# A graph-attention layer on one core: a table with its axes exchanged, set-up work in another order, and the last passes written out as a list

## The chip, the core and the metric

The kernel runs on one core of one Trainium2 chip. The engines of the core work side by side, each through its own queue in order: TensorE (PE; its weight loads are listed apart as PEld), VectorE (DVE), ScalarE (ACT), GpSimd (POOL) and SyncE (SP), which here only issues DMAs. The metric is the device time of one execution in microseconds (us), as the median of several runs.

## What is computed

The reference normalizes each of the 12,500 rows of x (128 numbers), lets each node look at its incoming edges (200,000 in all, sorted by target), keeps the 16 best-scored edges of a node, takes a softmax over them, and adds up the sources' rows with these weights:

```python
h = relu(layernorm(x))
Qv, Ku = h @ W_Q.T, h @ W_K.T
score = einsum('md,md->m', Qv[dst], Ku[src]) / sqrt(d) * exp(-edge_weight)
keep  = rank of the edge among those of its node < 16
w     = where(keep, exp(score - seg_max[dst]), 0)
alpha = w / segment_sum(w, dst)[dst]
agg   = segment_sum(alpha * (h[src] @ W_msg.T), dst)
out   = x + relu(h @ W_self.T + agg)
```

## The kernel before

**Groups.** The edges are cut into 112 groups (`G`) of 14 chunks of 128 edges (`GC` = 14; a 15th chunk is shared with the next group, `NJ` = 15). The last group, number 111, has 9 chunks. A group belongs to a window of at most 128 nodes. For each chunk POOL gathers 128 source rows with one indirect DMA into the tile `hs` (L176).

**Set-up (L278 to L421).** x is loaded in six pieces; DVE takes each row's statistics (`row_stats`, L194), ACT scales and clips each row block (`normed`, L215, the instructions of L220), and SP writes the piece to the table `h_tab` in DRAM (`finish`, L342). Only a complete `h_tab` can be gathered from. So that POOL need not wait for it, the first four groups (`RAW` = 4, "raw groups") are gathered from x itself (L339), and are normalized later in SBUF, inside the main loop (`raw_stats`, `raw_normed`). Before that the source indices must be turned from rows to columns: a copy (L335), PE transposes (L272), a cast into `idx_all` (L338). The groups from 4 on are gathered from `h_tab`; DVE copies two indices at a time (`let_go`, L183, the copy of L191) and POOL issues the two gathers.

**The places' table.** `pd` (L155) holds for each edge two numbers of 16 per group, the edge's place among its node's edges and its node's distance; its axes are (128 edges, group, 2, 16). DVE fills one half (L397), ACT the other (L400, L401). In each pass of the loop PE loads one group's 32 numbers as weights (L547, `edges_turned`); the copy `pdT` on ACT (L550) follows, and the matmuls into the same PSUM bank `a` (L534) wait for that copy.

**The loop (L712).** One pass `i` works on several groups at different stages, written out by hand: the scores of group `i` (PE `q_to_edges` L574, then DVE `scores` L583, `scores_in_slots` L591), the matrices for group `i+1` (`far_of`, `away`), the best 16 of group `i-2` (`slots_by_node` L599, `best`, `kept_to_edges` L642, `on_edges`), the weights and weighted sums of group `i-3` (`weights` L664, `sums` L674), the output of groups `i-4` and `i-5`. The calls `more(k)` between the stages are the `let_go` of later groups. The loop runs from -3 to `G + 5`; a stage whose group does not exist is left out. So the last seven passes (111 to 117) work the pipeline empty, in the same order as any other pass. An engine executes its instructions in the order in which the stages are written.

**Buffers that matter here.** `hs` has 8 buffers, `q` 3, the PSUM tiles `a`, `e`, `x` and `so` one each. `raw_stats` uses one set of small tiles for all raw groups.

Of the kernel before, what the change touches and what calls it, by code (L numbers as in the profile page):

```python
# [10 lines left out]
F32 = mybir.dt.float32  # L11
BF16 = mybir.dt.bfloat16
# [8 lines left out]
P = 128  # L21
# [35 lines left out]
def lead(j):  # L57
    return STEP * j - PRE
# [18 lines left out]
def gnn_layer(  # L77
# [35 lines left out]
    assert G > TAIL  # L113
# [41 lines left out]
    pd = const.tile([P, G, 2, 16], BF16, name="pd")  # L155
    dlw = pd[:, :, 1, 0:NJ]
# [58 lines left out]
    def normed(rows, n, rs, sm):  # L215

        nc.vector.reciprocal(rs, rs)
        nc.vector.scalar_tensor_tensor(sm, sm, -0.5, rs, op0=OP.mult, op1=OP.mult)
        for t in range(n):
            nc.scalar.activation(rows[:, t, :], rows[:, t, :], AF.Relu, bias=sm[:, t:t + 1],  # L220
                                 scale=rs[:, t:t + 1])

# [17 lines left out]
    with tc.tile_pool(name="edges", bufs=1) as ep, ExitStack() as stage:  # L240
# [48 lines left out]
        make_identity(nc, ident)  # L289
        nc.gpsimd.iota(dst_r, pattern=[[1, RL + P]], base=1 << 21, channel_multiplier=0)  # L290
# [3 lines left out]
        for p0, p1 in sixteens(1, k):  # L294
# [4 lines left out]
        nc.gpsimd.iota(slots, pattern=[[1, KM]], base=0, channel_multiplier=0,  # L299
                       allow_small_or_imprecise_dtypes=True)  # L300
        nc.gpsimd.iota(nvec, pattern=[[0, 1]], base=0, channel_multiplier=1,
                       allow_small_or_imprecise_dtypes=True)

        jj, eq = (alz[0][0:32, NJ * KM * k:NJ * KM * (k + 1)].rearrange("p (j k) -> p j k", k=KM) for k in range(2))
        nc.gpsimd.iota(jj, pattern=[[1, NJ], [0, KM]], base=0, channel_multiplier=0,
                       allow_small_or_imprecise_dtypes=True)
# [9 lines left out]
        nc.vector.memset(pd, 1.0)  # L316
        nc.vector.memset(dec_all[:, RR * CPR:CW], 0.0)
        nc.vector.tensor_scalar(minus, nvec, -1.0, None, op0=OP.mult)
        for j in range(NJ):
            nc.vector.memset(w0[:, j:j + 1], float(lead(j)))  # L320
# [8 lines left out]
        nc.vector.memset(alz[0], 0.0)  # L329
        for k in range(2):  # L330
            nc.vector.memset(sl1[k][:, :, KM:], 1.0)


        src_f = src_r.bitcast(F32)[:, 0:RW]
        nc.vector.tensor_copy(src_f, src_r[:, 0:RW])  # L335
        stat = {0: row_stats(prep, xs[0][2], sizes[0], "x0")}
        by_chunk = lambda t: t[:, 0:RR * CPR].rearrange("e (p j) -> e j p", j=CPR)
        to_columns(src_f, 0, lambda at, p: nc.vector.tensor_copy(at(by_chunk(idx_all)), p))  # L338
        for g in range(min(RAW, G)):  # L339
            gather_at_once(g, x)  # L340

        def finish(i):  # L342
            t0, n, xg = xs[i]
            normed(xg, n, *stat[i])
            for a, b in cuts:
                nc.sync.dma_start(by_part(h_tab)[a:b, t0:t0 + n, :], xg[a:b])

        for i in range(len(xs)):
            if i + 1 < len(xs):
                stat[i + 1] = row_stats(prep, xs[i + 1][2], sizes[i + 1], f"x{i + 1}", lambda: finish(i))  # L350
            else:
                finish(i)

# [28 lines left out]
        let_go(RAW, 2)  # L382
        nc.vector.memset(h0[:, 0:1], 0.0)
# [3 lines left out]
        let_go(RAW, 4)  # L387
        bb = rows_pool.tile([P, 2, G], F32, name="bb")
        nc.vector.tensor_copy(bb, pb[:, 0:2 * G].rearrange("p (a g) -> p a g", a=2))

        for j0 in range(0, NJ, 4):
            j1 = min(j0 + 4, NJ)
            pt = bank("q", 3)
            for j in range(j0, j1):
                nc.tensor.matmul(pt[:, (j - j0) * RR:(j - j0 + 1) * RR], lhsT=rel[:, j * P:(j + 1) * P],
                                 rhs=upper(ident[0:RR, 0:RR]), start=True, stop=True)
            nc.vector.tensor_tensor(dlw.rearrange("e g j -> e j g")[:, j0:j1, :],  # L397
                                    pt[:, 0:(j1 - j0) * RR].rearrange("e (j g) -> e j g", g=RR),
                                    bc(w0[:, j0:j1], RR), op=OP.subtract)
        to_columns(h1, HALO, lambda at, p: nc.scalar.copy(at(pd[:, :, 0, :].rearrange("e g j -> e j g")), p))  # L400
        nc.scalar.copy(pd[:, 0:G - 1, 0, GC:NJ], pd[:, 1:G, 0, 0:1])  # L401
# [30 lines left out]
    def all_checked():  # L432
# [15 lines left out]
        lambda: nc.vector.tensor_reduce(badc[:, 0:1], pd[:, :, 0, 0:NJ], axis=AX.XY, op=OP.max),  # L448
# [32 lines left out]
    with tc.tile_pool(name="win", bufs=2) as win:  # L481
# [23 lines left out]
        def raw_stats(g):  # L505
            T[g]["raw"] = row_stats(rows_pool, T[g]["hs"], own[g], "r")

        def raw_normed(g):
            normed(T[g]["hs"], own[g], *T[g]["raw"])


# [10 lines left out]
        def q_out(g):  # L522
            T[g]["q"] = win.tile([P, D], F32, name="q", bufs=3)
            nc.scalar.copy(T[g]["q"], so[:, P:2 * P])
# [20 lines left out]
        def edges_turned(g):  # L545
            pr = bank("a", 1)
            nc.tensor.matmul(pr[0:32, 0:P], lhsT=pd[:, g, :, :].rearrange("e w j -> e (w j)"), rhs=upper(ident),  # L547
                             start=True, stop=True)
            T[g]["pdT"] = win.tile([32, P], BF16, name="pdT")
            nc.scalar.copy(T[g]["pdT"], pr[0:32, 0:P])  # L550
# [161 lines left out]
        for i in range(-3, G + 6):  # L712
# [5 lines left out]
            if i + 1 < RAW:  # L718
                at(i + 1, raw_stats)

# [29 lines left out]
            if i + 1 < RAW:  # L750
                at(i + 1, raw_normed)
# [28 lines left out]
            at(i, scores_in_slots)  # L780
            more(6)
            at(i - 1, node_by_slots)
            at(i + 2, q_made)
            if i > 0 and later:
                later.pop(0)()
    assert not later
# [182 lines left out]
```

## Time and profile before

| | us |
|---|---|
| median of 10 runs | 2869.69 (2864.47 to 2878.52) |
| the profiled execution's own time | 2862.99 |
| its span, first to last instruction | 2861.2 |

| engine | busy us | share of the span | instructions |
|---|---|---|---|
| PE | 1946.3 | 68% | 13800 |
| PEld | 1546.9 | 54% | 13801 |
| DVE | 1278.9 | 45% | 6998 |
| ACT | 1053.4 | 37% | 2198 |
| POOL | 1498.6 | 52% | 1580 |

No engine is busy throughout. The rows with "idle before" tell what an engine waited for: the name after the arrow is the instruction whose signal came last, "remote" is a signal for which the profile shows no sender at that moment, and "issue" means that no wait is shown. A timeline row holds start, duration, engine, source line, operation and tiles, and behind it in brackets the idle time before. A row of windows holds a stretch of time and each engine's busy time in it, with the number of instructions, the granted PE clock as a share of the full one, the DMA engines' busy share and the rate in GB/s. The granted clock is 0.764 over the whole execution.

### The profile page before, as it was taken

To read this page: it belongs to the slowest core of one execution; us is meant where nothing else is said; L and a number is where in the kernel's file an instruction comes from. 1 tells how busy PE (TensorE), PEld (TensorE's weight loads), DVE (VectorE), ACT (ScalarE), POOL (GpSimd) and SP (SyncE) were. 2 spreads that over 40 slices of the span, in tenths; PEclk is the share of its full clock that TensorE was granted. 3 is DMA by queue.
4 is the path that set the end of the run, shared out by engine and by line. 5 is a ranking of instruction groups with operands and counts; after the bars stand their busy time and mean duration, and the time that the engine had idled before them with its cause. 6 is when DMAs were issued, how large, how long until landed. Compare 5 with 4: busy or idle time off the path is not lost. (4 is left out here: it accounts for less than half of the span.)

```text
span 2861.2 us, 42100 instructions
## 1 busy us (share of the span) xinstructions
PE 1946.3 (68%) x13800; PEld 1546.9 (54%) x13801; DVE 1278.9 (45%) x6998; ACT 1053.4 (37%) x2198; POOL 1498.6 (52%) x1580
## 2 busy tenths in 40 slices
PE   0257776776777767777776776776777777777676
PEld 0135555555555555555555555555555555555565
DVE  5436544444444444444444444444444444444445
ACT  5444333333333333333333333333333333333342
POOL 6634555555555555555555555555555555555520
PEclk9998777777777777777777777777777777777788
DMA  8211211111111111111111111111111111111110
GB/s 220 87 29 32 59 45 47 47 47 47 46 48 47 48 48 47 46 46 46 46 46 47 47 46 46 48 48 48 48 46 47 47 48 47 44 47 46 48 29 7
DMA packets 101472, 143.46 MB, mean 50 GB/s; under 512 B 31063, under 2 KB 74327, under 8 KB 100480
## 3 DMA queue, kind: packets, MB, share of 16 engines
q0 software_dynamic: 50144, 102.74, 12.6%
q1 hardware_dynamic: 51102, 37.99, 4.8%
q8 instruction: 108, 1.77, 0.3%
q14 instruction: 118, 0.97, 0.1%
HBM read 126.79 MB, written 14.40 MB: 49 GB/s over the span
## 5 line engine op out<-in xcount | busy, mean ns | idle before, releaser
L176 POOL DMA_INDIRECT hs<-h_tab,ix x1507 | 1433.1, 951 | 1234.2 <-DVE prod L583 579.0
L674 PE MATMUL a<-hs,alz 128*128 128x128 f32 x3348 | 594.3, 344 | 46.6 <-issue 43.8
L574 PEld LDWEIGHTS q<-q,to_e 128*128 128x128 f32 x3348 | 543.4, 242 | 133.1 <-issue 123.0
L534 PE MATMUL a<-rel,ident 112*128 112x512 bf16 (+1 forms) x447 | 181.4, 406 | 634.0 <-ACT far L536 580.2
L574 PE MATMUL q<-q,to_e 128*128 128x128 f32 x3348 | 591.2, 331 | 0.0
L536 ACT ACTIVATE far<-a,minus 128x512 bf16<-128x512 f32 (+1 forms) x447 | 295.2, 660 | 794.7 <-remote 590.1
L583 DVE SCALAR_TENSOR_TENSOR prod<-hs,dec_all,q 128x128 f32<-128x128 f32 x1674 | 483.2, 344 | 224.2 <-PE a L674 174.4
L674 PEld LDWEIGHTS a<-hs,alz 128*128 128x128 f32 x3348 | 547.3, 254 | 30.2 <-issue 21.6
L599 PEld LDWEIGHTS e<-opo,sl 128*41 128x41 f32 x3348 | 188.3, 140 | 679.5 <-issue 670.7
L613 DVE TENSOR_SCALAR ell<-slots,e 128x40 f32<-128x40 f32 x112 | 28.1, 251 | 1061.3 <-PE e L599 993.0
L559 ACT ACTIVATE aw<-a 128x400 bf16<-128x400 f32 x336 | 169.3, 504 | 231.1 <-PE a L557 213.7
L599 PE MATMUL e<-opo,sl 128*41 128x40 f32 x3348 | 230.2, 230 | 0.0
L557 PE MATMUL a<-minus_at,pdT 32*128 32x400 bf16 x336 | 164.8, 491 | 89.4 <-ACT aw L559 45.4
L679 ACT ACTIVATE agn<-a,rden 128x128 f32<-128x128 f32 x112 | 41.2, 368 | 443.4 <-PE a L674 438.6
L541 ACT ACTIVATE to_e<-far 128x1920 f32<-128x1920 bf16 x112 | 200.4, 1789 | 0.0
L583 DVE DVE_READ_ACCUMULATOR prod<-hs,dec_all,q 128x1 f32 x1674 | 137.9, 82 | 0.0
L563 ACT ACTIVATE opo<-aw 128x1200 f32<-128x1200 bf16 x112 | 136.0, 1215 | 0.0
L191 DVE COPY ix<-idx_all 128x2 int32<-128x2 int32 x754 | 135.1, 193 | 0.0
L642 PEld LDWEIGHTS <-to_e 128*128 128x128 bf16 x1674 | 66.9, 114 | 85.8 <-DVE prod L583 64.1
L550 ACT CAST pdT<-a 32x128 bf16<-32x128 f32 x112 | 28.5, 255 | 176.3 <-PE a L547 157.7
L591 DVE TENSOR_TENSOR sl<-opo,s 128x600 f32<-128x600 f32 x112 | 87.7, 783 | 3.8
L664 DVE TENSOR_TENSOR alz<-opo,kept 128x600 f32<-128x600 f32 x112 | 87.7, 783 | 3.9
(172 smaller groups left out, 1654.5 us busy)
## 6 DMA issues: line engine op xcount, KB each, us to landing
hs<-h_tab,ix POOLq DMA_INDIRECT x1507
h_r<-h_tab SPq DMA_DIRECT2D x112, 64.0 KB
x_t<-in_x_dram SPq DMA_DIRECT2D x108, 64.0 KB
out_dram<-o SPq DMA_DIRECT2D x108, 64.0 KB
xg<-in_x_dram SPq DMA_DIRECT2D x2, 1400.0 KB
h_tab<-xg SPq DMA_DIRECT2D x2, 1400.0 KB
xg<-in_x_dram SPq DMA_DIRECT2D x1, 1120.0 KB
h_tab<-xg SPq DMA_DIRECT2D x1, 1120.0 KB
```

The source lines that it names most:

```text
L176: nc.gpsimd.indirect_dma_start(out=T[g]["hs"][:, j, :], out_offset=None, in_=table[0:N, :], in_offset=bass.IndirectOffsetOnAxis(ap=index(j ...
L191: nc.vector.tensor_copy(ix[:, j0:j1], idx_all[:, GC * g + j0:GC * g + j1])
L534: nc.tensor.matmul(pr[:, 0:n1 - n0], lhsT=upper(ident[0:RR, g:g + 1]).to_broadcast([RR, P]), rhs=rel[:, n0:n1], start=True, stop=True)
L536: nc.scalar.activation(T[g]["far"][:, n0:n1], pr[:, 0:n1 - n0], AF.Square, bias=minus)
L541: nc.scalar.activation(T[g]["to_e"][:, 0:n], T[g]["far"][:, 0:n], AF.Relu, bias=1.0, scale=-1.0)
L557: nc.tensor.matmul(pr[:, 0:400], lhsT=T[g]["pdT"], rhs=minus_at.rearrange("k w j s -> k (w j s)")[:, n0:n1], start=True, stop=True)
L559: nc.scalar.activation(T[g]["aw"][:, n0:n1], pr[:, 0:400], AF.Square)
L563: nc.scalar.activation(T[g]["opo"].rearrange("e w j s -> e (w j s)"), T[g]["aw"], AF.Relu, bias=1.0, scale=-1.0)
L574: nc.tensor.matmul(pq[:, (j - j0) * P:(j - j0 + 1) * P], lhsT=T[g]["to_e"][:, j * P:(j + 1) * P], rhs=T[g]["q"], start=True, stop=True)
L583: nc.vector.scalar_tensor_tensor(prod, rows_of(g, j), dec_all[:, c:c + 1], T[g]["pq", b][:, (j % 4) * P:(j % 4 + 1) * P], op0=OP.mult, op1 ...
L599: nc.tensor.matmul(et[0:KM + 1, STEP * j:STEP * j + WN], lhsT=sl1[g % 2][:, j, :], rhs=T[g]["ow"][:, j, :], start=False, stop=(j == n - 1))
L674: nc.tensor.matmul(T[g]["pa"][:, 0:P], lhsT=alz[g % 2][:, WW * j + PRE:WW * j + PRE + P], rhs=rows_of(g, j), start=(j == 0), stop=(j == n ...
```

## The change

1. `pd` becomes (128 edges, 32, group): one number of all groups lies side by side, and one group's 32 numbers lie 224 bytes apart. Only the two columns that need a value beforehand are set to one, and the last group's missing places to zero.
2. In the set-up the `iota` instructions for `slots`, `nvec` and `jj` come before that of `dst_r`; the copy of the source indices is split in two; the statistics of x's first piece come after the casts to `idx_all` and the raw gathers; the fills of `w0`, `alz[0]` and `sl1` come after the last piece of x.
3. The statistics of raw groups 0 and 1 are taken right after the last piece of x, and their norming on ACT goes behind two later `let_go`. The statistics of raw groups 2 and 3 move to the end of pass 0, with the norming of the first chunk of each; the other 13 chunks are normed at the end of passes 1 and 2.
4. `q` has 2 buffers.
5. The loop ends after pass 110. Passes 111 to 117 are one list of stages (`L` = 111) in a new order.

```diff
-    pd = const.tile([P, G, 2, 16], BF16, name="pd")
-    dlw = pd[:, :, 1, 0:NJ]
+    pd = const.tile([P, 32, G], BF16, name="pd")
+    dlw = pd[:, 16:16 + NJ, :].rearrange("e j g -> e g j")
...
-    def normed(rows, n, rs, sm):
+    def normed(rows, n0, n1, rs, sm):
-        nc.vector.reciprocal(rs, rs)
-        nc.vector.scalar_tensor_tensor(sm, sm, -0.5, rs, op0=OP.mult, op1=OP.mult)
-        for t in range(n):
+        if n0 == 0:
+            nc.vector.reciprocal(rs, rs)
+            nc.vector.scalar_tensor_tensor(sm, sm, -0.5, rs, op0=OP.mult, op1=OP.mult)
+        for t in range(n0, n1):
...
+    def raw_stats(g):
+        T[g]["raw"] = row_stats(rows_pool, T[g]["hs"], own[g], f"r{g % 2}")
+    def raw_normed(g):
+        normed(T[g]["hs"], 0, own[g], *T[g]["raw"])
+    def raw_begun(g):
+        normed(T[g]["hs"], 0, 1, *T[g]["raw"])
+    def raw_finished(g):
+        normed(T[g]["hs"], 1, own[g], *T[g]["raw"])
...
-        nc.vector.memset(pd, 1.0)
+        for k in (15, 31):
+            nc.vector.memset(pd[:, k, :], 1.0)
+        nc.vector.memset(pd[:, GC:NJ, G - 1:G], 0.0)
...
-        nc.vector.tensor_copy(src_f, src_r[:, 0:RW])
-        stat = {0: row_stats(prep, xs[0][2], sizes[0], "x0")}
+        nc.vector.tensor_copy(src_f[:, 0:4 * P], src_r[:, 0:4 * P])
+        nc.vector.tensor_copy(src_f[:, 4 * P:], src_r[:, 4 * P:RW])
         to_columns(src_f, 0, lambda at, p: nc.vector.tensor_copy(at(by_chunk(idx_all)), p))
-        for g in range(min(RAW, G)):
+        for g in range(RAW):
             gather_at_once(g, x)
+        stat = {0: row_stats(prep, xs[0][2], sizes[0], "x0")}
...
+        for j in range(NJ):
+            nc.vector.memset(w0[:, j:j + 1], float(lead(j)))
+        nc.vector.memset(alz[0], 0.0)
+        for k in range(2):
+            nc.vector.memset(sl1[k][:, :, KM:], 1.0)
+        for g in range(2):
+            raw_stats(g)
...
         let_go(RAW, 2)
+        raw_normed(0)
...
         let_go(RAW, 4)
+        raw_normed(1)
...
-            nc.tensor.matmul(pr[0:32, 0:P], lhsT=pd[:, g, :, :].rearrange("e w j -> e (w j)"), rhs=upper(ident),
+            nc.tensor.matmul(pr[0:32, 0:P], lhsT=pd[:, :, g], rhs=upper(ident),
...
-        for i in range(-3, G + 6):
+        for i in range(-3, G - 1):
...
-            if i + 1 < RAW:
-                at(i + 1, raw_stats)
...
-            if i + 1 < RAW:
-                at(i + 1, raw_normed)
...
             at(i, scores_in_slots)
+            if i == 0:
+                raw_stats(2)
+                raw_stats(3)
+                raw_begun(2)
+                raw_begun(3)
+            if i in (1, 2):
+                raw_finished(i + 1)
...
+        q_to_edges(L, 0)
+        output(L - 5)
+        store(L - 5)
+        weights(L - 3)
+        turned(L - 4)
+        all_slots(L - 1)
+        slots_out(L - 1)
+        best(L - 2)
+        sum_of_exps(L - 2)
+        q_to_edges(L, 1)
+        node_by_slots(L - 1)
+        to_rows(L - 4)
+        all_sums(L - 3)
+        kept_to_edges(L - 2)
+        best(L - 1)
+        sum_of_exps(L - 1)
+        scores(L, 0)
+        kept_on_edges(L - 2)
+        turned(L - 3)
+        kept_to_edges(L - 1)
+        scores(L, 1)
+        weights(L - 2)
+        all_sums(L - 2)
+        to_rows(L - 3)
+        for b in range(2, blocks):
+            q_to_edges(L, b)
+            scores(L, b)
+        scores_in_slots(L)
+        to_nodes(L)
+        kept_on_edges(L - 1)
+        turned(L - 2)
+        best(L)
+        sum_of_exps(L)
+        weights(L - 1)
+        kept_to_edges(L)
+        all_sums(L - 1)
+        to_rows(L - 2)
+        kept_on_edges(L)
+        turned(L - 1)
+        weights(L)
+        all_sums(L)
+        to_rows(L - 1)
+        turned(L)
+        to_rows(L)
```

The new helpers put old stages together: `turned` is `sums_turned` and `sums_turned_out`; `all_slots` the three parts of `slots_by_node`; `to_nodes` is `all_slots`, `slots_out` and `node_by_slots`; `kept_on_edges` is `one_over_sum`, `on_edges` and `exps`; `all_sums` both parts of `sums` and `sums_out`; `to_rows` is `products`, `output` and `store`.

## The prediction

> **What bounds the kernel now.** I read the stretches of the span first, then the costliest groups, then the waits, then the timeline of the first 235 us and of the last 40. The stretches, with the busy time of PE, PEld, DVE, ACT and POOL in each:
>
> ```profile
> 12.00:100.00 88.00, 7.16 (x37) 5.54 (x37) 44.15 (x173) 43.17 (x109) 55.73 (x56) 1.00 0.69 192
> 100.00:147.00 47.00, 15.07 (x51) 8.73 (x52) 17.59 (x74) 26.04 (x40) 34.11 (x34) 1.00 0.22 62
> 221.00:235.00 14.00, 12.36 (x118) 9.94 (x118) 11.54 (x55) 8.44 (x17) 0.02 (x1) 1.00 0.04 11
> 235.00:2741.00 2506.00, 1785.42 (x12662) 1421.22 (x12661) 1106.20 (x6183) 895.89 (x1852) 1368.27 (x1442) 0.74 0.16 47
> 2811.00:2849.00 38.00, 26.14 (x243) 23.89 (x242) 19.34 (x90) 4.61 (x20) 4.22 (x4) 0.91 0.03 10
> ```
>
> 2506 of 2861 us are 103 ordinary passes (4 to 106) of 24.3 us. Their code is untouched but for the weights load of the places' table. One pass without gathers (221 to 235) took 14.0. The difference is seen in the groups:
>
> ```profile
> L176 POOL DMA_INDIRECT hs<-h_tab,ix x1507 | 1433.1, 951 | 1234.2 <-DVE prod L583 579.0
> L536 ACT ACTIVATE far<-a,minus 128x512 bf16<-128x512 f32 (+1 forms) x447 | 295.2, 660 | 794.7 <-remote 590.1
> ```
>
> ACT loses 590 us at L536, 105 times some 5.6 us: PE's matmuls for it are done by 1507, but the signal comes at 1512.3, 1.1 us after POOL's eighth gather in a row ended (1511.2). The same shows at 146.56 below, 1.7 us after a row of gathers that ended at 144.9. So I read a pass as POOL's: 14 gathers at 1.25 us spacing are 17.5 us, the rest are POOL's pauses. The change touches neither, so its worth lies before 235 us and after 2811. The rows there:
>
> ```profile
> 2.71 3.04 DVE L316 MEMSET pd<- 128x3584 bf16 x1 [0.69 <-issue]
> 9.69 2.06 DVE L329 MEMSET alz<- 128x2400 f32 x1 [0.57 <-DMA xg<-in_x_dram]
> 14.55 2.82 DVE L338 CAST idx_all<-q 128x448 int32<-128x448 f32 x4
> 15.75 1.12 POOL L176 DMA_INDIRECT hs<-in_x_dram,idx_all  x1 [9.57 <-DVE idx_all L338]
> 81.75 0.25 DVE L217 RECIPROCAL rsx<-rsx 125x15 f32<-125x15 f32 x1 [12.29 <-remote]
> 88.33 2.46 POOL L176 DMA_INDIRECT hs<-in_x_dram,idx_all  x1 [0.30 <-issue]
> 97.25 7.46 DVE L397 TENSOR_TENSOR pd<-q,w 128x448 bf16<-128x448 f32 x4
> 100.73 0.95 POOL L176 DMA_INDIRECT hs<-h_tab,ix  x1 [9.94 <-issue]
> 102.39 7.06 ACT L400 CAST pd<-q 128x448 bf16<-128x448 f32 x4 [7.09 <-issue]
> 108.92 1.01 ACT L401 COPY pd<-pd 128x111 bf16<-128x111 bf16 x1
> 122.06 5.48 ACT L220 ACTIVATE hs<-hs,smr,rsr 128x128 f32<-128x128 f32 x14
> 146.56 0.35 DVE L583 SCALAR_TENSOR_TENSOR prod<-hs,dec_all,q 128x128 f32<-128x128 f32 x1 [10.41 <-remote]
> ```
>
> And one row of the waits between 100 and 235 us (total, times, longest), with three of the last passes:
>
> ```profile
> PE a L557 <- ACT aw L559: 20.8, 6, 5.4
> ...
> 2817.11 3.59 PE L674 MATMUL a<-hs,alz 128*128 128x128 f32 x30
> 2826.17 4.80 PE L674 MATMUL a<-hs,alz 128*128 128x128 f32 x30
> 2834.90 5.22 PE L674 MATMUL a<-hs,alz 128*128 128x128 f32 x30
> ```
>
> The reader is to see: raw gathers start at 15.75 and end at 90.8; the first gather from `h_tab` waits until 100.73 for the table; group 0's scores wait until 146.56; and the norming of a raw group (5.48) sits between two ACT copies for which PE waits.
>
> **Indices first.** SP's queue, which reuses the semaphores of the four source loads, goes on at 6.8 to 8.7, so the indices are there by 8.7; DVE copies them at 11.71, behind the zeroing of L329. Without it (2.06) and without L316 (3.04), and with 512 of 1792 columns copied first (1.07 x 512/1792 = 0.31), the casts start at about 9.9 instead of 14.55 and the gathers at 11.1: 4.6 earlier, ending near 86. That is no gain by itself: what follows is the table. It is complete when ACT has normed x's six pieces and SP's last write has landed. ACT works at 1.4 us spacing from 51 to 92, while POOL gathers without pause, instead of the 0.39 of L220's 5.48 for 14. If POOL ends 4.6 earlier, ACT's last five rows run fast; but POOL also starts earlier to slow it. I take -3 for the first gather from `h_tab`, bounds -5 (all of it follows) and +4 (the slowing also moves forward). On POOL the three small `iota` (0.98 together) now hold up that of `dst_r`; SP loads over it only at 34.3, so nothing waits.
>
> **DVE and ACT before the loop.** DVE gets, behind x's last reciprocal, two sets of statistics (each 14 x 0.2 = 2.8 and six small ones, 108.06 to 111.77 = 3.7), the zeroing of 2.06 and 17 small fills of some 0.06: 10.5 more. It loses most of L397: 448 numbers side by side cost about 0.6, nearest row the 512 of L536 at 0.69, so 2.4 for four against 7.46: -5. ACT gets two normings, 11.0 more, filling an idle stretch of 7.1 before L400, and loses 7.06 - 2.5 at L400 and 0.8 at L401. By this the last of these tables (`dec_all`, 114.1 before) is done at about 117: +3 (0 to +5). Pass -1 then lacks its norming (-5.5), so group 0's scores could start earlier than before by 2.5; but they start when POOL pauses, 34 gathers after the first from `h_tab` (100.73 + 44 = 144.9). So only the -3 above counts here; the rest has that wait as cover, some 10 us. SP's queue keeps its order, but its writes of `h_tab` and loads of nodes follow the same table.
>
> **Passes 0 to 3.** The wait row of 100 to 235 us gives PE 20.8 us behind L559, the norming in the way: 5.2 of it in pass -1, under the cover just named, 15.6 in passes 0 to 2. PE waits for ACT's `pdT`, which stood behind the statistics' square root, 21.2 us in the same window, of which one wait of 14.4 is the late signal: 6.8 more. Removed: 22.4. Added: behind pass 0 the DVE work of two groups (7.4) stands before two square roots and two rows on ACT, and `pdT` of the next pass behind these, with about 2 us of PE work ahead of the wait: 7. DVE's `let_go` for the next pass are queued behind it, so POOL pauses too. Behind passes 1 and 2, 13 rows of 0.39 each = 5.1, of which 1.5 is ACT's usual idle time before `pdT`: 3.5 each. Added: 14. Sum -8.5, bounds -16 (the late signals hide what is added) and 0 (what was removed was hidden, what is added is not).
>
> **The turned table in the passes.** L547 loads 32 numbers in 92 ns; now each is 224 bytes from the next. The trace shows no such load. Below: nothing, it can't fall. Above: L401 reads and writes with wide steps, 9.1 ns a number, L400 writes so, 3.9; the difference of 5.2 x 32 = 0.17 us, 112 times 19 us. I take 0: the load comes before the late signal of its pass, which POOL ends, so a small delay has 5 us of cover. L430 and L444 read the table once each with the same steps, at most 1680 x 5.2 ns = 8.7 us on DVE, which waits 10.4 in each pass for L599. Two `q` buffers cost nothing: PE reads a `q` a pass before ACT overwrites it.
>
> The Trainium skill speaks against this edit (SBUF — State Buffer, section on the DMA port swizzle): it has 16-byte lines and says that each access that crosses to a new line pays. No row here shows that for weights; it gives no price, and if it meant the 0.17 above the sum would be 19 higher.
>
> **The last passes.** From the start of pass 111 (2810.9) to the end of the last store (2848.9) are 38.0. I put both orders together from rows at PE's quick speed: `sums` 3.6 (2.2 for group 111), `best` 2.0, `on_edges` with its reciprocal 2.5 (2.0), `weights` 1.0 (0.7), four scores 1.15. Old order: `sums`(109) ends at 19.5, `best`(111) at 23.5, `sums`(110) at 27.6 with `on_edges`(111) under it, `sums`(111) at 31.5, store at 34.9. New order: `best`(110) and `sums`(108) earlier (7.4, 8.6), `weights`(109) 13.7, `sums`(109) 17.3; but DVE's output of 108 stands before the last scores of 111, so these end at 18.7, `on_edges`(110) at 21.8, `best`(111) 23.8, `weights`(110) 24.8, `sums`(110) 28.5, output of 109 at 29.4, and only then `on_edges`(111) 31.4, `weights` 32.1, `sums` 34.3, store 37.7. That is 2.8 later; what both lack to 38.0 is slow PE after idle time (4.80 and 5.22 for 3.59) and the POOL queue. I take +3, bounds -1 (the new order keeps PE quick) and +6 (three slow sums).
>
> **Sum.** -3 - 8.5 + 0 + 3 = -8.5 against the profiled execution's 2863.0 = 2854.5. That execution lay 6.7 under the median of the runs shown, so for a median I say 2861.
>
> **Rivals.**
> 1. The weights load becomes dear (other side). Place L547, price up to +19, 2880; it decides from 0.13 us a pass, where 2861 + 14.4 passes 2875.4. For: ACT's and DVE's wide steps cost two to three times (L397, L401). Against: 5 us of cover in each pass. 0.12.
> 2. The set-up's gain is hidden: the table's completion and POOL's 56 gathers to group 7 set the time until pass 3. Then 0 and the list's +3: 2873. For: 146.56 follows POOL. Against: the 15.6 us lie after that point. 0.24.
> 3. The list is better than I worked out, because PE stays quick and DVE overtakes: PE's 26.1 busy us and 4 for the last output would make 30 instead of 38, so 2861 - 3 - 8 = 2850. For: idle PE in a third of the stretch. Against: the chain above. 0.14.
> 4. The passes' phase against the late signals shifts, as 22.6 to 26.5 us long passes show: 0.1 us in 103 passes is +-10, 2851 or 2871. 0.08.
>
> The forecast (2853 to 2869) has 0.42. 0.2% is about what a measurement of this kernel can tell from no change: 2864.0 to 2875.4 is the same. Faster: 0.34 of the forecast, 0.14 of rivals 3 and half of 4 = 0.52. Same: 0.08 of it and 0.18 of rival 2 = 0.26. Slower: rival 1, 0.06 of rival 2, half of 4 = 0.22. The range 2845 to 2879 leaves the dearest loads and the best list out.
>
> **What would show it.** First raw gather near 11; first from `h_tab` at 96 to 99; L397's four in 2.5 us; passes 4 to 106 at 24.3; L547's load at 0.09 to 0.12; group 3's scores done near 223.5 instead of 235; the last store 41 us after the start of group 111's first matmul. It would be wrong if passes 4 to 106 differ by 0.1 us, or if group 0's scores start later than 147.

## The result, and the profile after

The changed kernel takes 2880.46 us (median of 18 runs, 2873.06 to 2894.7) where the kernel before took 2869.36 beside it (61 runs): a ratio of 1.0043, 95% interval 1.0032 to 1.0054. It is slower by 11.1 us; the forecast was faster by 8.5 and the range ended at 2879. The profiled execution has a span of 2876.3 us where that of before had 2861.2.

The stretches of the span (start:end, length, then busy time and instructions of PE, PEld, DVE, ACT and POOL, the PE clock, the DMA share, GB/s), the first two at the same times as before, the others cut at the same places of the work:

```profile
12.00:100.00 88.00, 2.36 (x8) 1.74 (x8) 40.04 (x218) 43.16 (x111) 53.05 (x56) 1.00 0.69 191
100.00:147.00 47.00, 16.78 (x70) 11.18 (x71) 15.57 (x49) 24.69 (x52) 37.02 (x33) 1.00 0.21 59
236.00:2749.00 2513.00, 1800.51 (x12670) 1435.26 (x12668) 1107.53 (x6188) 895.89 (x1854) 1368.64 (x1442) 0.73 0.16 47
2818.00:2864.00 46.00, 32.61 (x248) 29.61 (x247) 19.31 (x91) 5.19 (x22) 3.96 (x4) 0.74 0.03 8
```

The reader is to see that no stretch became shorter: the end of pass 3 moved from 235 to 236, the passes' stretch grew from 2507 (235 to 2742) to 2513, and the last passes, 38.0 from group 111's first matmul to the last store before, now need 45.4 (2818.65 to 2864.02), with more PE busy time (32.6 for 26.1) at a lower clock (0.74 for 0.91). The two groups shown of before changed little, so a pass is built as it was:

```profile
L176 POOL DMA_INDIRECT hs<-h_tab,ix x1507 | 1439.8, 955 | 1241.0 <-DVE prod L598 593.3
L551 ACT ACTIVATE far<-a,minus 128x512 bf16<-128x512 f32 (+1 forms) x447 | 295.1, 660 | 808.6 <-remote 617.6
```

Rows of the timeline (start, duration, engine, line, operation, tiles, idle time before) that answer to those of before:

```profile
10.41 1.12 POOL L176 DMA_INDIRECT hs<-in_x_dram,idx_all  x1 [4.05 <-DVE idx_all L349]
...
98.40 0.15 DVE L191 COPY ix<-idx_all 128x2 int32<-128x2 int32 x1
98.53 1.19 DVE L399 CAST dst_r<-dst_r 112x1984 f32<-112x1984 int32 x1
98.82 2.29 POOL L176 DMA_INDIRECT hs<-h_tab,ix  x1 [14.28 <-DVE ix L191]
99.76 1.22 DVE L401 TENSOR_SCALAR rel<-dst_r 112x1920 bf16<-112x1920 f32 x1
101.33 2.09 DVE L405 TENSOR_TENSOR src_r<-dst_r 112x1855 f32<-112x1855 f32 x1
101.42 2.82 POOL L176 DMA_INDIRECT hs<-h_tab,ix  x1 [0.30 <-issue]
103.46 4.02 DVE L407 TENSOR_TENSOR_SCAN h<-src_r 112x1856 f32<-112x1856 f32 x1
104.55 3.69 POOL L176 DMA_INDIRECT hs<-h_tab,ix  x1 [0.31 <-issue]
108.11 2.09 DVE L419 TENSOR_TENSOR pd<-q,w 128x448 bf16<-128x448 f32 x4
108.54 0.95 POOL L176 DMA_INDIRECT hs<-h_tab,ix  x1 [0.30 <-issue]
...
155.70 0.69 ACT L551 ACTIVATE far<-a,minus 128x512 bf16<-128x512 f32 x1 [6.91 <-remote]
157.23 0.94 POOL L176 DMA_INDIRECT hs<-h_tab,ix  x1 [6.70 <-DVE ix L191]
```

The raw gathers start 5.3 us earlier (15.75 before) and the table's DVE writes take 2.09 instead of 7.46 (forecast 2.5). But the first gather from `h_tab` is only 1.9 earlier, it now waits for DVE's copy at 98.40, and the first three gathers take 2.29, 2.82 and 3.69 where others take 0.95, each beside a long DVE instruction. The fourth starts at 108.54 where before it started at 104.48. POOL then gathers to 150.5 without a pause, and at 155.70 ACT goes on after 6.9 us of idle time that ended with a signal of no shown sender. Such waits, "remote" in the rows, are called late signals here as in the prediction.

The weights load of the table, before (L547) and turned (L562; ns: min/median/max), and the last passes' `sums`:

```profile
L547 PEld LDWEIGHTS <-pd x112: 92/92/102, 115.0 to 2796.9; 128*32 128x32 bf16 x112
L547 PE MATMUL a<-ident,pd x112: 230/230/290, 115.0 to 2796.9; 128*32 128x128 bf16 x112
L562 PEld LDWEIGHTS <-pd x112: 134/135/138, 120.2 to 2804.5; 128*32 128x32 bf16 x112
L562 PE MATMUL a<-ident,pd x112: 217/273/324, 120.2 to 2804.5; 128*32 128x128 bf16 x112
```

```profile
2823.14 3.51 PE L689 MATMUL a<-hs,alz 128*128 128x128 f32 x30
2831.53 6.06 PE L689 MATMUL a<-hs,alz 128*128 128x128 f32 x30 [2.24 <-DVE alz L679]
2844.45 6.41 PE L689 MATMUL a<-hs,alz 128*128 128x128 f32 x30 [0.39 <-DVE alz L679]
```

The load takes 135 ns where it took 92 before, its matmul 273 where it took 230. Two of the long `sums` take 6.1 and 6.4 us instead of 3.5.

### The profile page after: what moved, and what is told of

It is laid out like the page before. It is cut to its first block, busy times and chain, and to the rows that moved or that the text cites. A ratio compares the mean times of both kernels' runs of the same rounds, so it can differ in the third digit from the quotient of the medians.

```text
span 2876.3 us, 42113 instructions
## 1 busy us (share of the span) xinstructions
PE 1968.1 (68%) x13800; PEld 1567.8 (55%) x13801; DVE 1274.4 (44%) x7001; ACT 1048.0 (36%) x2198; POOL 1502.6 (52%) x1580
## 5 line engine op out<-in xcount | busy, mean ns | idle before, releaser
L549 PE MATMUL a<-rel,ident 112*128 112x512 bf16 (+1 forms) x447 | 182.0, 407 | 661.2 <-ACT far L551 605.8
L589 PEld LDWEIGHTS q<-q,to_e 128*128 128x128 f32 x3348 | 549.7, 244 | 119.7 <-issue 104.8
L589 PE MATMUL q<-q,to_e 128*128 128x128 f32 x3348 | 598.3, 334 | 0.0
L551 ACT ACTIVATE far<-a,minus 128x512 bf16<-128x512 f32 (+1 forms) x447 | 295.1, 660 | 808.6 <-remote 617.6
L689 PEld LDWEIGHTS a<-hs,alz 128*128 128x128 f32 x3348 | 554.8, 257 | 31.2 <-issue 19.0
L572 PE MATMUL a<-minus_at,pdT 32*128 32x400 bf16 x336 | 165.2, 492 | 57.0 <-ACT aw L574 30.1
```

What stands on the lines that cost most here:

```text
L549: nc.tensor.matmul(pr[:, 0:n1 - n0], lhsT=upper(ident[0:RR, g:g + 1]).to_broadcast([RR, P]), rhs=rel[:, n0:n1], start=True, stop=True)
L551: nc.scalar.activation(T[g]["far"][:, n0:n1], pr[:, 0:n1 - n0], AF.Square, bias=minus)
L572: nc.tensor.matmul(pr[:, 0:400], lhsT=T[g]["pdT"], rhs=minus_at.rearrange("k w j s -> k (w j s)")[:, n0:n1], start=True, stop=True)
L589: nc.tensor.matmul(pq[:, (j - j0) * P:(j - j0 + 1) * P], lhsT=T[g]["to_e"][:, j * P:(j + 1) * P], rhs=T[g]["q"], start=True, stop=True)
L689: nc.tensor.matmul(T[g]["pa"][:, 0:P], lhsT=alz[g % 2][:, WW * j + PRE:WW * j + PRE + P], rhs=rows_of(g, j), start=(j == 0), stop=(j == n ...
```

## The experiments

The first eight runs, e17 and the comparison above fell on chips where the kernel before takes 2863 to 2870. The others fell on three chips where it takes 2059 to 2061; what those show is told last, since a pass takes 17 us there instead of 24.3. Three places are read from each profile: when the scores of a group are multiplied into slots ("group 0's scores", "group 4's"), the length from group 4's to group 106's ("passes 4 to 106"), and from group 110's to the end of the span ("the end"). Figures in brackets behind a ratio are its 95% interval.

**Parts of the change taken back or made alone.** e1 takes back part 5, the list:

```diff
-        for i in range(-3, G - 1):
+        for i in range(-3, G + 6):
...
-        q_to_edges(L, 0)
...
-        to_rows(L)
```

> The changed kernel with the old last passes in place of the list. Theory A (the list itself costs about 7 us: from the scores of group 110 to the end the changed kernel took 58.9 us where the kernel before took 51.5, with two sums of 6.1 and 6.4 us): about 2873, 1.0015 times before, and 51 to 52 us from group 110's scores to the end. Rival (the list is no worse; its end fell on a bad stretch of TensorE's clock that any order would meet): 2880, 1.004, and 57 us or more.

Measured: 1.0028 [1.0012, 1.0044], 4 us less than the changed kernel in ratio; the end takes 54.7 us, with two `sums` at 6.3 and 6.2. Between the two forecasts: the list costs about 4 by this run, and slow `sums` at the end also meet the old order.

e2 takes back part 1, the table's layout, but keeps its smaller fill:

```diff
-    pd = const.tile([P, 32, G], BF16, name="pd")
+    pd = const.tile([P, G, 2, 16], BF16, name="pd")
...
+        nc.vector.memset(pd[:, :, :, 15:16], 1.0)
...
-            nc.tensor.matmul(pr[0:32, 0:P], lhsT=pd[:, :, g], rhs=upper(ident),
+            nc.tensor.matmul(pr[0:32, 0:P], lhsT=pd[:, g, :, :].rearrange("e w j -> e (w j)"), rhs=upper(ident),
```

> The changed kernel with the table laid out by group as before (its writes in the set-up at the old price, its fill of ones cut to the one column that needs it). Theory A (the weights load of the turned table, 0.134 us where it was 0.092, and its matmul, 0.273 where it was 0.230, lengthen each pass by 0.045 us): passes 4 to 106 some 4.6 us shorter in all, time about 2876, 1.0023 times before. Rival (the 0.045 us a pass come from where the passes fall against the gathers, not from the load): the load goes back to 0.092 and the time stays at 2880.

Measured: 1.0019 [1.0006, 1.0032]; the load is back at 92 ns, passes 4 to 106 take 2481.8 us, 6.6 less than in the changed kernel. e3 is part 1 alone in the kernel before:

> The kernel before with the turned table alone. Theory A: passes 4 to 106 some 4.6 us longer, the shorter table writes in the set-up (5 us on VectorE, 5.4 on ScalarE) hidden by the gathers: 2874, 1.0016 times before. Rival 1 (the load costs nothing by itself): 2869, 1.000. Rival 2 (the set-up's saving is on the path): first scores 5 us earlier, 2864 to 2869.

Measured: 1.001 [0.9996, 1.0025]; passes 4 to 106 take 2492.9, 9.0 more than before; group 0's scores 1.9 earlier, group 4's 1.5 later. e4 is part 5 alone:

> The kernel before with the list of the last stages alone. Theory A (the list costs 7 us by itself): 2876.5, 1.0025 times before, 58 us or so from group 110's scores to the end, sums of 110 and 109 at 6 us each. Rival (only +3, as I worked out with TensorE quick): 2872, 1.001. Rival 2 (nothing or a gain): 2866 to 2869.

Measured: 1.0015 [0.9998, 1.0032]; the end takes 55.0, 3.4 more than before.

From these and the later profiles: with the table turned, passes 4 to 106 take 2486.2, 2486.4, 2488.4 and 2492.9 us; with it by group 2478.6, 2481.6, 2481.8, 2483.6, 2483.9 and 2484.8 (e8, which adds work to the passes, left out). The means differ by 6.1, 0.06 us a pass, and the two sets don't overlap. The end takes 55.0, 55.1, 56.5 and 59.0 with the list, 51.5, 51.6, 51.7, 51.7 and 54.7 with the old order: 4.1 more.

e5 is part 2 alone (with e2's smaller fill), e6 part 3 alone (with two `q` buffers):

```diff
         to_columns(src_f, 0, lambda at, p: nc.vector.tensor_copy(at(by_chunk(idx_all)), p))
         for g in range(min(RAW, G)):
             gather_at_once(g, x)
+        stat = {0: row_stats(prep, xs[0][2], sizes[0], "x0")}
```

> The kernel before with the indices ahead of x's first statistics and the fills and zeroings moved behind x's norming, nothing else. My prediction's -3: 2864, ratio 0.999, first gather from h_tab at 96 to 99, scores of group 4 done 3 us earlier (255 instead of 258). Rival (the gathers end earlier, but the table of h and the fills moved behind it take it back): the raw gathers end at 85, the first gather from h_tab is at 98 to 101, scores of group 4 unchanged within the 2 us by which three runs of this set-up differ, ratio 1.000.

Measured: 0.9973 [0.9956, 0.9990], faster than both kernels. The raw gathers end at 83.8, the first gather from `h_tab` is at 96.0, group 0's scores are at 157.3, group 4's at 250.9. e6:

```diff
+        for g in range(2):
+            raw_stats(g)
...
+            if i == 0:
+                raw_stats(2)
+                raw_stats(3)
```

> The kernel before with only the statistics and the norming of the raw groups moved. My prediction's -8.5 for passes 0 to 3: 2860, ratio 0.997, scores of group 3 done near 226, of group 4 near 250. Rival (three runs of the changed set-up have group 4's scores at 261, 267 and 265 where three with the old one have 259, 260 and 256: the moved work is on the path, what was removed had been under the gathers): group 3 at 237, group 4 at 262 to 265, ratio 1.0015 to 1.0025, 2871 to 2873.

Measured: 1.000 [0.9985, 1.0014]. Group 3's scores at 234.3, group 4's at 259.3: neither my 8.5 us nor the rival's loss.

The parts don't add up: 0.9973, 1.000, 1.001 and 1.0015 make 0.9998 in sum, and all together measured 1.0043. Where the first passes stand in each profile (us from the span's start):

```
                         raw gathers  first from  28th from   group 0's  group 4's
                         end          h_tab       h_tab ends  scores     scores
before                   90.8         100.7       137.4       166.2      258.5
e3 table                 94.1          99.9       135.3       164.3      260.0
e4 list                  97.2          97.5       132.1       162.4      256.3
e7 awake at the end      95.8          96.1       130.8       161.3      255.1
e8 awake in passes       96.3          96.6       131.3       162.1      257.8
e5 indices               83.8          96.0       134.3       157.3      250.9
e6 norming               89.7          98.9       140.4       163.8      259.3
changed                  84.5          98.8       140.5       165.6      261.1
e1 changed, old end      85.2          99.6       141.2       166.4      266.6
e2 changed, old table    87.0          98.4       140.3       165.1      264.8
e17 changed, row cut     84.4          98.4       140.1       165.2      261.5
```

Two things stand out. The first is that the first gather from `h_tab` does not always wait for the table. SP's first load from `h_tab` (`h_r`) waits for the table's writes; it goes on at 99.92 before, at 99.05 in e3 and at 95.17 in e5, and POOL's gather follows 0.8 us later. In e4, e7 and e8, whose set-up is that of before, it goes on at 84.04, 81.27 and 78.83, and the gather follows the last raw gather instead (rows of e4; the last two belong to a later paragraph):

```profile
84.04 0.39 SPq L497 DMA_DIRECT2D h_r<-h_tab  x1
96.23 0.95 POOL L176 DMA_INDIRECT hs<-in_x_dram,idx_all  x1 [0.30 <-issue]
97.48 0.94 POOL L176 DMA_INDIRECT hs<-h_tab,ix  x1 [0.30 <-issue]
...
138.68 0.94 POOL L176 DMA_INDIRECT hs<-h_tab,ix  x1 [0.30 <-issue]
146.19 0.35 DVE L583 SCALAR_TENSOR_TENSOR prod<-hs,dec_all,q 128x128 f32<-128x128 f32 x1 [14.81 <-remote]
```

In the changed kernel, e1, e2 and e17 it waits for DVE's index copy, at 98.0 to 99.2. So with the same set-up the table is complete up to 21 us earlier in one profile than in another.

The second: with the norming moved (the last five rows) the 28th gather ends at 140.1 to 141.2, 7 us later than the mean of the old order (133.4 over the five rows above e5). e2 and e5 differ up to pass 4 in the norming and the number of `q` buffers alone, and group 4's scores by 13.9. Profiles with the same first passes differ here by up to 3.3 us (before, e4, e7) and 5.5 (changed, e1).

**The row of gathers.** After group 5's last gather the changed kernel goes on gathering until 150.5, while e5's POOL waits for an index copy that DVE has behind the statistics:

```profile
97.23 3.56 POOL L176 DMA_INDIRECT hs<-h_tab,ix  x1 [0.30 <-issue]
...
134.37 0.18 DVE L206 TENSOR_TENSOR dmr<-str 128x14 f32<-128x14 f32 x1 [9.56 <-issue]
137.01 0.50 ACT L562 ACTIVATE aw<-a 128x400 bf16<-128x400 f32 x1 [5.47 <-issue]
138.61 0.94 POOL L176 DMA_INDIRECT hs<-h_tab,ix  x1 [4.35 <-DVE ix L191]
```

In e5 (timeline of the stretch) DVE, which had stood still for 9.6 us, goes on at 134.37, just as POOL's row ends, and ACT at 137.01. e17 puts such a pause into the changed kernel; e12 and e15 are the same kernel:

```diff
+                if i == 0 and k < 4:
+                    for m in range(4 if k == 3 else 0):
+                        let_go(6, m)
+                    return
                 if i in (-1, 0, 1):
                     g = i + 6
```

> e12 once more. Where the kernel before takes about 2860, theory B (the long row of gathers holds the others up): GpSimd pauses at 139.5 after group 5, group 0's scores at 157 to 160, group 4's at 253 to 260, ratio 1.0015 to 1.003. Rival (the row only fills time in which the others wait for something else): group 0 at 165, group 4's at 264 or later, ratio 1.0045 or more. Where it takes 2059: 0.999 to 1.0015, as in e12 and e15.

Measured: 1.0045 [1.0025, 1.0065], group 0's scores at 165.2: the rival's numbers, though group 4's are at 261.5, between the two forecasts. Its timeline:

```profile
142.60 0.26 ACT L565 CAST pdT<-a 32x128 bf16<-32x128 f32 x1 [10.84 <-issue]
142.76 0.95 POOL L176 DMA_INDIRECT hs<-h_tab,ix  x1 [2.66 <-DVE prod L598]
153.25 0.35 DVE L598 SCALAR_TENSOR_TENSOR prod<-hs,dec_all,q 128x128 f32<-128x128 f32 x1 [10.55 <-issue]
155.31 0.69 ACT L551 ACTIVATE far<-a,minus 128x512 bf16<-128x512 f32 x1 [10.44 <-remote]
```

ACT's `pdT` goes on 2.5 us after the row ends (it was at 145.83 in the changed kernel), but POOL pauses for only 2.66 us, and DVE and ACT stand still again until its next eight gathers are over. So a short cut gains nothing. Nor does a pause let the others go on by itself: in e4 (rows above) and e7 POOL's row ends at 139.62 and 138.34, and group 0's scores wait until 146.19 and 145.06 with no gather running. e18, which takes all of group 6's gathers out of the stretch, was to tell a pause that is too short from waits of another kind:

```diff
+                if i == 0:
+                    for m in range(7 if k == 5 else 0):
+                        let_go(6, m)
+                    return
                 if i in (-1, 0, 1):
                     g = i + 6
```

> The changed kernel with all of group 6's index copies, and so its fourteen gathers, moved behind group 0's third set of scores; e17 had left GpSimd a pause of 2.7 us only, after which ten gathers came in a row and the others stood still again. Theory B (it is the gathers that hold the others up): GpSimd pauses from 140 to about 151, no other engine waits over 5 us between 143 and 152, group 0's scores at 153 to 158, group 4's at 252 to 258, ratio 1.000 to 1.002. Rival (the others would wait there anyway): group 0's at 164 or later, ratio 1.004. Rival 2 (pass 0 is quick, but the gathers moved back hold up pass 1 as much): group 0's at 153 to 158, group 4's at 261 or later, ratio 1.004. Where the kernel before takes 2059, GpSimd alone sets the time: ratio 1.001 to 1.006.

It fell on a chip where the kernel before takes 2059 (1.0007 [0.9997, 1.0016]), so this stays open.

**PE kept busy.** e7 puts work without a use into the last three waits of the old order, e8 into passes 4 to 105:

```diff
+        def awake(n):
+            for _ in range(n):
+                nc.tensor.matmul(so[:, 0:P], lhsT=ident, rhs=ident, start=True, stop=True)
...
+            if i >= G - 1 and i - 2 < G:
+                awake(8)
             at(i - 2, kept_to_edges)
```

> The kernel before with eight matmuls of the identity with itself, 2 us of work whose result nothing reads, ahead of the last three kept_to_edges, where TensorE waits 1.7, 2.1 and 2.5 us for best. If its idle time there is what makes the next sums slow (4.80 and 5.22 us where others take 3.6): three sums at 3.6, the last passes 3 us shorter, 48 to 49 us from group 110's scores to the end, ratio 0.999. Rival (the low clock follows a load or a beat of its own): sums as before at 4.8 to 6, the end unchanged or up to 2 us later.

Measured: 0.9982 [0.9962, 1.0002]; the end takes 48.4 instead of 51.6, and the long `sums` are as quick as others:

```profile
2812.89 3.59 PE L674 MATMUL a<-hs,alz 128*128 128x128 f32 x30
2821.77 3.59 PE L674 MATMUL a<-hs,alz 128*128 128x128 f32 x30
2829.29 3.59 PE L674 MATMUL a<-hs,alz 128*128 128x128 f32 x30
```

PE's granted clock (the number behind POOL's) is half in the kernel before beside its `sums` of 4.80, and full in e7 throughout the last passes:

```profile
2825.28:2828.70 3.42, 3.09 (x27) 3.09 (x28) 2.57 (x10) 0.42 (x3) 0.00 (x0) 0.50 0.00 0
2803.60:2841.00 37.40, 32.08 (x318) 29.41 (x317) 21.91 (x98) 5.08 (x22) 3.54 (x4) 1.00 0.03 10
```

```diff
+            if 4 <= i < G - 6:
+                awake(12)
             at(i + 1, far_of, 3)
```

> The kernel before with twelve such matmuls (2.9 us at the quick clock) in each of passes 4 to 105, ahead of the last far_of, where TensorE waits 5 us for the late signal. If idle time makes the clock fall and the slow work lies on the passes' path: clock 0.85 or more in the passes and passes of 23 us instead of 24.3, some 130 us in all, ratio 0.955. Rival (the passes are bound by the gathers and their pauses, whatever TensorE's clock): clock up, passes at 24.3, ratio 1.000. Rival 2 (the added work is on the path): passes up to 2.9 us longer, ratio up to 1.10.

Measured: 1.0018 [1.0002, 1.0034]. The clock in the passes rises from 0.74 to 0.85, their length stays (2485.9 from group 4 to 106, 2483.9 before): on this kind of chip a quicker clock on PE does not shorten a pass.

**On the other chips.** Here the kernel before takes 2059 to 2061. 

> The kernel before with two parts: the indices first and the norming moved, table and last passes as before. Alone the one gave 0.9973, the other 1.000. Theory B (the two undo each other: with the norming out of pass -1 VectorE copies group 6's indices early, GpSimd gathers without a pause until 147 to 150, and the other engines stand still with it): scores of group 0 at 164 to 166, of group 4 at 262 to 266, ratio 1.000 to 1.0015. Rival (the parts add up): group 0 at 157, group 4 at 251 to 253, ratio 0.9975.

Measured 1.001 [1.000, 1.002].

> The changed kernel with the norming back in the passes as before; indices first, turned table and list stay. Theory B: group 0's scores at 157 to 159, group 4's at 251 to 255, some 10 us less than the changed kernel, ratio to before 1.000. Rival (what the changed kernel lost in its first passes comes from the turned table's quicker writes or from elsewhere): group 4 at 261 or later, ratio 1.003 to 1.0045.

Measured 1.0005 [0.9996, 1.0014]; repeated as e14 and e16: 1.0019 [1.0009, 1.0028] and 1.0017 [1.0007, 1.0027].

> The kernel before with the indices first and the idle matmuls ahead of the last three kept_to_edges: the two parts that gained. If they add up: group 4's scores at 251, 48 us from group 110's scores to the end, ratio 0.9955 to 0.9965. If not: 0.9975 or the 51.7 us at the end that the indices alone had.

Measured 1.0001 [0.9991, 1.0012].

> The changed kernel with the copies of group 6's first eight index columns, and so their gathers, moved behind group 0's first four scores. Theory B (the long row of gathers holds the others up): GpSimd pauses at 139.5 after group 5, ScalarE's pdT of pass 0 at 141 instead of 145.8, group 0's scores at 157 to 160, group 4's 4 to 8 us earlier than in the changed kernel, ratio to before 1.0015 to 1.003. Rival (the row only fills time in which the others wait for something else; fewer gathers are done by then and must follow later): group 0 at 165, group 4 at 264 or later, ratio 1.0045 or more.

Measured 0.9994 [0.9982, 1.0005], repeated as e15: 1.0014 [1.0004, 1.0025].

> The changed kernel itself, beside the two that each alter one part of it. Where the kernel before takes about 2860: ratio 1.0043 as before, group 4's scores at 261 to 267, 55 to 59 us from group 110's scores to the end. Where it takes 2059, as in the last four runs, in which nothing stood still while GpSimd gathered: only the list is left of the loss, 8 us at the end, and the ratio is 1.000 to 1.004.

Measured 1.0008 [0.9999, 1.0017]: the changed kernel costs nothing here that can be told. Its page:

```profile
L176 POOL DMA_INDIRECT hs<-h_tab,ix x1507 | 1444.6, 959 | 471.3 <-issue 302.8
...
L551 ACT ACTIVATE far<-a,minus 128x512 bf16<-128x512 f32 (+1 forms) x447 | 294.9, 660 | 369.4 <-PE a L549 359.6
```

A gather takes as long as above (959 ns for 955), but POOL is idle for 471 us instead of 1241, and ACT's "remote" waits at L551 (617.6 us in the changed kernel above) are gone. Passes 4 to 106 take 1737 to 1744 us, 17 a pass, in all of them, with the table turned (1737.6 to 1743.9) or not (1737.4 and 1744.0): POOL gathers through, and the means (1740.6 and 1740.7) don't differ, so 0.06 us more on PE is not seen there. None of these runs tests what the first passes lose on the slower chips; the end with the list is 55.4 to 60.0 here too, 51.6 with the old order (e9) and 49.3 with e11's added matmuls.

They show one gain: with the indices first, group 4's scores are at 198.3 and 198.4 us where the table is by group (e11, e9), and at 189.4 to 191.3 where it is turned (e10, e13, e14, e16), with the norming moved or not. Up to there e9 and e13 differ by the table alone, as do e11 and e10. So the quicker set-up of the turned table is worth some 8 us on these chips, about what the list costs at the end.

## Why the prediction was wrong

**Indices first: -3 to the first gather from `h_tab`.** The first raw gather came at 10.41 (11 forecast) and the first from `h_tab` at 98.82, inside my 96 to 99. Alone (e5) the part is worth 7.7 us by its ratio, more than I gave it. The step I wrote can't be told from one profile: e5's first gather from `h_tab` is 4.7 earlier than in the profile of before (95.99), but e4, e7 and e8 have it at 96.1 to 97.5 with the old order. What sets e5 apart comes after the 28th gather: from there to group 0's scores it needs 23 us, the old order 29 to 31.

**DVE and ACT before the loop: 0, "the rest has that wait as cover".** This is the step that failed. I counted 10.5 us more on DVE before the loop and took the last table to be done 3 us later (it was 5: `dec_all` ended at 119.3). What I did not follow is who is queued behind the statistics on DVE: the copy for the first gather from `h_tab` (98.40), and four long instructions (1.19, 1.22, 2.09, 4.02). In the profile of before these run ahead of the first gather from `h_tab`, and only a later one, L404, meets the fourth:

```profile
83.50 1.26 DVE L379 CAST dst_r<-dst_r 112x1984 f32<-112x1984 int32 x1
86.67 1.22 DVE L381 TENSOR_SCALAR rel<-dst_r 112x1920 bf16<-112x1920 f32 x1 [1.82 <-issue]
87.89 2.08 DVE L384 TENSOR_TENSOR src_r<-dst_r 112x1855 f32<-112x1855 f32 x1
92.96 4.02 DVE L386 TENSOR_TENSOR_SCAN h<-src_r 112x1856 f32<-112x1856 f32 x1 [2.91 <-remote]
104.48 2.90 POOL L176 DMA_INDIRECT hs<-h_tab,ix  x1 [0.30 <-issue]
```

Now they lie beside the first three. The second and third end 0.8 us after the long instruction that they meet: 101.42 + 2.82 against 101.33 + 2.09, 104.55 + 3.69 against 103.46 + 4.02. The three take 8.80 us for 2.85, and so POOL's row, begun 1.9 us earlier, is 3.1 behind by its 28th gather (140.53 for 137.40). I had reckoned 44 us for 34 gathers, as in the profile of before. What the first 28 gathers take beyond 0.945 each adds up to 6.8 to 7.2 us in each of the five profiles with the norming moved, to 0.0 to 2.0 in the old order and 3.5 in e5, while the waits between them stay at 0.30: this is the whole of the 7 us. The cost could be read before: the raw gather at 88.33, a row of the prediction, takes 2.46 beside the comparison of L384.

I also let group 0's scores start when POOL pauses. The pause moved back from 144.9 to 150.5, with 36 gathers, not 34, in the row, and the scores after the first four followed it by 5.2 us (155.72), where before it was 1.7 (146.56) and in e4 6.6: they came after the row's end, but that alone does not set them. By group 0's scores the five are 2.0 us behind the mean of the old order (165.2 for 163.2), since from the 28th gather they need 23.4 to 25.1 us, the old order 28.8 to 30.8. That two groups are no longer normed in there would explain it, but e5, which still norms them there, needs 23.0.

The Trainium skill has a rule that would explain this (SBUF — State Buffer, "Who interferes with whom", and the warning on DVE and DMAs issued by GpSimd above it): VectorE and GpSimd share one pair of SBUF ports under an exclusive lock, and while VectorE holds it, GpSimd can't write the descriptors of its DMAs. The rows above agree, with gathers of 2.29 to 3.69 us for 0.95. For an operation on two tensors the section says two things: with both inputs in SBUF it contends with a GpSimd instruction that reads SBUF, and it is inferred to leave such descriptors alone. A gather reads its row indices from SBUF (`ix`); the one beside the comparison at L405, whose two inputs lie in SBUF, took 2.82, which fits the first.

**Passes 0 to 3: -8.5.** What I said would go went: PE's waits behind ACT's `aw` fell from 20.8 us to 5.0 between 100 us and the end of pass 3:

```profile
PE a L572 <- ACT aw L574: 5.0, 5, 3.8
```

What I said would come came to the tenth: waits for `pdT` of 7.00, 3.47 and 3.58 where I wrote 7, 3.5 and 3.5. But one of the waits that went, pass 0's (3.51 in the profile of before), lies ahead of group 0's scores. From there to group 3's it is 16.9 that go (5.03 and 5.38 behind `aw`, 2.33 and 4.15 for `pdT`) for 14 that come, 3 and not 8.5. Measured, the five profiles with the norming moved take 70.5 to 71.8 us there, the others 68.7 to 70.7: 2 longer. Part of what was removed was replaced at once: in pass 1 a late signal of 3.84 us stands at the same wait (5.03 before), and in pass 0 one of 7.2 stands in front of L549. My lower bound had this as a phrase ("the late signals hide what is added"); it went the other way, they hid what was removed. Which instruction each late signal is for I can't read, so the rest is not assigned.

**The turned table: 0, "a small delay has 5 us of cover".** Mis-sized. The load takes 0.135 us, 0.043 over 0.092, its matmul 0.043 more, and passes 4 to 106 grew by 0.06 each: 6 us in all, 3 to 7 by the ratios of e3 and e2. So the 5 us of cover were not there. My reading, which no run tries, is that PE's chain ahead of the late signal is on the path too. This is rival 1 with its place right and its price a third of the upper bound; the point from which I let it decide, 0.13 us a pass, was reckoned as if nothing else went wrong. A step of 224 bytes made the load dearer by 1.3 ns a number (43 ns over 32), not by the 5.2 that I took from ACT.

**The last passes: +3, bounds -1 to +6.** Right in size, half by luck: 4.1 by the profiles' means, 4 by the ratio of e1, 3.4 by e4's profile. The 3 were for the order of the stages with PE quick. But in e4 three `sums` lose 4.8 us against their quick time (6.19, 4.85 and 3.22 for 3.59, 3.59 and 2.27), in the kernel before two lose 2.8. So 2.0 of e4's 3.4 are slower `sums`, and some 1.4 are left for the order.

**Sum.** Instead of -3 - 8.5 + 0 + 3: about +5 to group 4's scores (262.7 for 257.5, means of five profiles each), +6 in the passes and +4 at the end. That is 15, what the two profiled executions differ by; the medians differ by 11, and single profiles of the same passes scatter by 3 to 6 us. Of my own marks, group 0's scores did start before 147 (141.70), but the next four came only at 155.72: the mark was set at the wrong instruction. Group 3's scores were done at 237.0, not near 223.5. Passes 4 to 106 stayed within its 0.1 us and yet cost 6 in sum.

Shown: that the turned table costs its part (ten profiles, and the ratio of e2), that the list costs its part (nine profiles; the intervals of e1 and e4 leave it open), and that the indices alone gain. What the norming costs beside them rests on e2 against e5: 13.9 us by group 4's scores, and by the ratios (1.0019 and 0.9973, less 4 us for the list) an estimate of 9, give or take 6. That the 7 us up to the 28th gather are longer gathers is read from eleven profiles; that they are long because of DVE's instructions beside them agrees in all, but was not tried by itself. Why e5 needs 6 us less than the old order after the 28th gather stays open: its pause of 4.35 us fits, but e17's of 2.66 did not bring it, e4 and e7 have one of 8 without it, and the run that would have told fell on another kind of chip.

## What to carry to other kernels

Work moved into an engine's idle time also moves what is queued behind it: follow the next instructions of that queue until one that another engine waits for, and look at what they will now run beside. By these profiles, long VectorE instructions on tensors in SBUF should be over before a row of gathers starts, or stand beside one that nothing waits for. Parts that each gain or cost nothing can lose together, so measure the likeliest part alone as well as the whole: here the indices first, by themselves, beat both kernels (0.9973).

## What the runs showed that was not expected

- The same kernel takes 2863 to 2870 us on some chips (medians) and 2059 to 2061 on others. With gathers equally long (0.96 us), the changed kernel has late signals on a slower one (617.6 us in all at L551) and none there on a quicker one. No run shows the cause.
- Idle time of 2.1 to 2.5 us on PE ahead of `sums` at the end goes with 1.2 to 2.8 us more in them (1.7 us of it did not); eight matmuls without a use in each of three such waits took the end from 51.6 to 48.4 us, with 3.59 for each of the `sums` and the clock at 1.00 for 0.50. The Trainium skill (TensorE: Matmul & The Clock Gate, part 1) has the clock halved after an idle window of some 3.4 us and restored by a busy one: the halved clock and the remedy are seen here, but the waits are shorter than that window. In passes 4 to 105 twelve such matmuls raised the clock from 0.74 to 0.85 and gained nothing.
- A weights load of 32 bf16 numbers that lie 224 bytes apart takes 135 ns, side by side 92.
